# A graph transformer layer and a graph attention layer: three projections by 26 block products instead of three times seven

## The chip, the core and the metric

The kernel runs on one core of a Trainium2 chip. The core has five engines that each work through their own queue of instructions in order and signal each other by semaphores: TensorE (PE, matmuls from SBUF into PSUM; the profile shows its weight loads apart as PEld), VectorE (DVE), ScalarE (ACT), GpSimd (POOL) and SyncE (SP, which here issues nearly all DMAs). The time is device microseconds of one execution, the median of several runs.

## What is computed

128 graphs of 128 nodes with 512 features, all in fp32. Layer 0 normalises, projects to query, key and value, attends over 8 heads with scores that are multiplied by the adjacency matrix, and projects back. Layer 1 is a graph attention layer over the same adjacency. Cut to what matters:

```python
# layer 0
h = jnp.maximum(_layernorm(x), 0.0)
q, k, v = (proj(Wq, bq), proj(Wk, bk), proj(Wv, bv))   # h @ W.T + b, 8 heads of 64
scores = jnp.einsum('bhqd,bhkd->bhqk', q, k) * SCALE
scores = scores * (adj + adj)[:, None, :, :]
ctx = jnp.einsum('bhqk,bhkd->bhqd', softmax(scores), v)
x = x + ctx @ Wo.T + bo
# layer 1
h = jnp.maximum(_layernorm(x), 0.0)
Wh = h @ W
e = leaky_relu(Wh @ a[:512] + (Wh @ a[512:]).T, 0.2)
attention = softmax(where(adj > 0.5, e, -9e15), axis=1)
x = x + elu(attention @ Wh)
```

## The kernel before

Batches (graphs) go in pairs, `p` from 0 to 63, and for the projections in groups `g` of two pairs, four batches. `hA` holds the group's normalised, rectified inputs with features on the partitions, in four blocks: two halves of the tokens (one pair each) by two halves of the features. Each of the products q, k and v is a 2x2 by 2x2 block product by Winograd's scheme: 7 products instead of 8 (`PRODUCTS`, L130), each of 4 matmuls of 256 columns (L258). VectorE forms the sums of weight blocks once (`weight_sum`, L137) and the sums of token blocks for each group (`hidden_sum`, L226, through `token_sum`, L148). The results gather in PSUM banks a, b and c; ScalarE copies a first part out, with the bias for q and k (`firsts`, L281), and VectorE adds the others (`adds`, L285, at L279). The two output projections use the same scheme by rows (`product_rows`, L291).

Around the products, per batch: scores (L320, on half the rows of the TensorE array at a time), weighting by adjacency (L327), maxima, exponentials and shares on VectorE and ScalarE, a blockwise transpose (L355) that goes through DRAM and back (L359, L365), and the context (L388, on half the columns of the array). Per pair: output projection, addition to x (L402), statistics (L165), layer 1 with its two dot products per batch (L425), gathering (L481), projection, elu and store (L511, L515, L521). `hidden` (L217) subtracts the mean and multiplies by the inverse deviation, both read as rows that were sent through DRAM. `shift` (L231) adds a constant row to x.

All work is recorded in an order that is written out by hand: `HEAD`, then `ORDER` once per pair, then `TAIL` are lists of step names with a pair or a lag (L564 to L650), and `steps` (L680) gives each name its function. No scheduler moves anything: each engine runs its instructions in the order in which the steps stand. Step names that matter below: `U`, `F`, `A` the 21 products and their firsts and adds; `hs` the token sums; `hd0`, `hd1` the two halves of `hidden`; `sh` the shift; `cs`, `gs` the token sums of the context `cxT` and of the gathered `gT`; `sca`, `scb` the scores of a pair's two batches and `pca`, `pcb` their contexts. All PSUM tiles come from one pool of 8 banks, taken in turn (L57).

Of the kernel before, what the change touches and what calls it, by code (L numbers as in the profile page):

```python
# [24 lines left out]
def kernel(  # L25
# [6 lines left out]
    wqT: bass.AP,  # L32
    bq: bass.AP,
    wkT: bass.AP,
    bk: bass.AP,
    wvT: bass.AP,
# [23 lines left out]
    xs, x0s, adjs, adjTs, hAs, hSs = {}, {}, {}, {}, {}, {}  # L60
# [18 lines left out]
    def half_of_hidden(p):  # L79

        g, i = divmod(p, 2)
        if g not in hAs:
            hAs[g] = grp.tile([P, 4, 2, 2 * S], F32, name="hA")
        return hAs[g][:, 2 * i : 2 * i + 2].rearrange("p q c k -> p (q c) k")
# [19 lines left out]
    def column(src, name):  # L104
# [10 lines left out]
    wv_sb, wq_sb, wk_sb, wo_sb, w1_sb = (  # L115
        const.tile([P, 7, 2, E // 2], F32, name=name) for name in ("wv", "wq", "wk", "wo", "w1")
    )
# [16 lines left out]
    FIRSTS = {0: (0, 0), 2: (1, 0), 4: (1, 1), 5: (0, 1)}  # L134
    ADDS = {1: (0, 0, "b"), 4: (1, 1, "c"), 6: (1, 0, "c")}
# [12 lines left out]
    def token_sum(h, s, k):  # L148

        if k == 0:  # L150
            nc.vector.tensor_tensor(s[:, 0], h[:, 2], h[:, 3], OP.add)
        elif k == 1:
            nc.vector.tensor_tensor(s[:, 1], s[:, 0], h[:, 0], OP.subtract)  # L153
        elif k == 2:
            nc.vector.tensor_tensor(s[:, 2], h[:, 0], h[:, 2], OP.subtract)
        else:
            nc.vector.tensor_tensor(h[:, 2], h[:, 1], s[:, 1], OP.subtract)
# [59 lines left out]
    def hidden(p, k):  # L217

        h = hAs[p // 2][:, 2 * (p % 2) : 2 * (p % 2) + 2].rearrange("p q c k -> p (q c) k")
        row = rows0[p][:, None, :, k].to_broadcast([P, 2 * 2, 2 * S])  # L220
        if k == 0:
            nc.vector.tensor_tensor(h, h, row, OP.subtract)
        else:
            nc.vector.scalar_tensor_tensor(h, h, 0.0, row, op0=OP.max, op1=OP.mult)

    def hidden_sum(g, k):  # L226
        if g not in hSs:
            hSs[g] = grp.tile([P, 3, 2, 2 * S], F32, name="hS")
        token_sum(hAs[g], hSs[g], k)

    def shift(p):  # L231


        nc.vector.tensor_tensor(xs[p], xs[p], c_sb[:, None, :].to_broadcast([P, 2, E]), OP.add)

    accs = {}

    def product(g, which, n):

        if n == 0:  # L240
            if which == "v":
                vs[g] = grp.tile([P, G, E], F32, name="v")
            else:
                qks[g, which] = {}
        if which != "v" and n in (0, 2):
            qks[g, which][n // 2] = grp.tile([P, C, 2 * S], F32, name=which + "T", bufs=3 if which == "q" else 2)
        w = {"q": wq_sb, "k": wk_sb, "v": wv_sb}[which]
        ha, wb, bank = PRODUCTS[n]
        fresh = (g, which, bank) not in accs
        if fresh:  # L250
            accs[g, which, bank] = ps1.tile([P, 2, 2 * S], F32, name="acc_" + bank, tag="ps1")
        acc = accs[g, which, bank]
        h = hAs[g][:, ha] if ha < 4 else hSs[g][:, ha - 4]
        for m in range(2):
            ms = slice(m * P, (m + 1) * P)
            for c in range(2):
                lhsT, rhs = (h[:, c, ms], w[:, wb, c, :]) if which == "v" else (w[:, wb, c, ms], h[:, c, :])
                nc.tensor.matmul(  # L258
                    acc[:, m, :], lhsT, rhs, start=fresh and m == 0 and c == 0, stop=c == 1, skip_group_check=True
                )  # L260

        def dst(t, f):
            if which == "v":
                return vs[g][:, 2 * t : 2 * t + 2, f * 2 * P : (f + 1) * 2 * P]
            return qks[g, which][t][:, 2 * f : 2 * f + 2, :]

        def first(t, f):
            a = accs[g, which, "a"]
            if which == "v":
                nc.scalar.copy(dst(t, f), a)  # L270
            else:
                bias = bk_sb if which == "k" else bq_sb
                for m in range(2):
                    j = 2 * f + m
                    nc.scalar.activation(dst(t, f)[:, m, :], a[:, m, :], AF.Identity, bias=bias[:, j : j + 1])  # L275

        def add(t, f, bank):
            d = dst(t, f)
            nc.vector.tensor_tensor(d, accs[g, which, bank], d, OP.add)  # L279

        def firsts():  # L281
            if n in FIRSTS:
                first(*FIRSTS[n])

        def adds():  # L285
            if n in ADDS:
                add(*ADDS[n])

        return firsts, adds
# [20 lines left out]
    def scores(b):  # L310
        p, i = divmod(b, 2)
        g, h = divmod(p, 2)
        qT, kT = qks[g, "q"][h], qks[g, "k"][h]
# [80 lines left out]
    def keep_context(b):  # L394
        nc.scalar.copy(rows_of(cxT, b % 2), pcs.pop(b))
# [88 lines left out]
    def keep_gathered(p, i):  # L484
        if p not in gTs:
            gTs[p] = work.tile([P, 7, 2, S], F32, name="gT")
        nc.scalar.copy(rows_of(gTs[p], i), pgs.pop((p, i)))  # L487
# [77 lines left out]
    SEQ = "v0 v1 v2 v3 v4 q0 v5 q1 v6 q2 q3 q4 k0 q5 k1 q6 k2 k3 k4 k5 k6".split()  # L565
# [6 lines left out]
    EARLY, LATE = 3, 4  # L572

    def listed(text, mark):
# [3 lines left out]
        lx@0 lx@1 Lq1@0 Lq0@0 lx@2 Lk0@0 Lk1@0 Lv0@0 t1@-5 Lo0@0 t0@-5 pp@0 hn0@0 hn1@0 tp0@0 t0@-4 tp1@0 ev0@0 ev1@0  # L578
        t1@-4 U6@-2 Wq0@0 pp@1 Wq1@0 t1@-3 U8@-2 hn0@1 l0@-2 Wq2@0 Lv1@0 hn1@1 tp0@1 Lo1@0 U3@-1 Lw1@0 t0@-3 ev0@1 Lu@0
        Wq3@0 pp@2 tp1@1 hn1@2 U5@-1 ev1@1 hn0@2 F6@-2 Wk0@0 hs0@-3 F3@-1 U1@-2 Wk1@0 hs1@-3 hs2@-3 U10@-2 tp0@2 F10@-2  # L580
        U7@-1 t1@-2 t0@-2 U2@-1 Wv0@0 F7@-1 pp@3 Wk3@0 F1@-2 A8@-2 ev0@2 U9@-1 hn0@3 Wv1@0 hn1@3 hs3@-3 tp0@3 l0@-1
        tp1@2 Wv2@0 la@-1 U3@-2 ev1@2 Lw0@0 ev0@3 lt@0 F9@-1 tp1@3 F2@-1 ccp@0 F3@-2 ev1@3 U1@0 ccd@0 t0@-1 t1@-1 U4@-2
        Wo0@0 l0@0 s0@-1 cu10@0 U5@-2 Wv3@0 A5@-1 U4@-1 hs0@-1 U10@-1 U1@-1 F10@-1 F4@-1 ccs@0 A2@-1 cch@0 sca@0 Wk2@0
        scb@0 ata0@0 ata1@0 U6@-1 mxa@0 hs1@-1 exa2@0 U3@1 t1@0 F5@-2 exa3@0 A6@-1 U6@0 A5@-2 F1@0 Wo1@0 rca1@0 t0@0
        U9@-2 F6@0 l0@1 s0@0 exa1@0 f0@0 exa0@0 U3@0 A9@-2 nma3@0 Wo2@0 nma2@0 rca0@0 cu01@0 U10@0 nma1@0 nma0@0 hs2@-1
        F3@1 U8@0 fla@0 Ww0@0 bla@0 U8@-1 atb0@0 la@0 atb1@0 mxb@0 U5@1 A8@0 exb2@0 A9@-1 pla@0 U2@-2 exb0@0 A5@1 exb1@0
        sh@0 F10@0 U11@-1 exb3@0 rcb1@0 U7@-2 nmb3@0 A11@-1 rcb0@0 t0@1 t1@1 U2@1 F7@-2 nmb1@0 cu11@0 l0@2 s0@1 nmb2@0
        f0@1 U7@1 F3@0 lT@0 cu00@0 nmb0@0 lT@1 sca@1 A2@-2 flb@0 scb@1 pca@0 F7@1 ata0@1 blb@0 ata1@1 F2@1 U5@0 mxa@1
        hs3@-1 exa0@1 U9@1 t1@2 exa1@1 Ww2@0 plb@0 exa3@1 t0@2 U1@1 exa2@1 hd0@0 s0@2 F9@1 la@1 U4@1 l0@3 pea@0 rca0@1
        sh@1 hd0@1 U8@1 F4@1 rca1@1 nma1@1 nma0@1 U10@1 A9@1 nma3@1 nma2@1 F5@0 fla@1 o0@0 F10@1 o1@0 atb0@1 bla@1 U4@0  # L590
        atb1@1 mxb@1 pcb@0 od0@0 exb3@1 A5@0 exb0@1 hd1@0 sca@2 pla@1 exb2@1 U9@0 A2@1 exb1@1 Wo3@0 peb@0 rcb0@1 od1@0
        nmb0@1 cs0@0 U11@1 cs1@0 nmb1@1 rcb1@1 cs2@0 nmb2@1 Ww1@0 nmb3@1 cs3@0 o2@0 U2@0 od2@0 flb@1 U6@1 ata0@2 blb@1
        ata1@2 mxa@2 o4@0 o3@0 exa1@2 od4@0 A2@0 exa3@2 U6@2 A6@1 plb@1 exa2@2 od4c@0 hd1@1 o6@0 F6@2 f0@2 hs0@1 o5@0
        exa0@2 A9@0 sup0@0 A11@1 U1@2 rca0@2 od6@0 nma1@2 od5@0 hs2@1 sup1@0 rca1@2 st0@0 nma3@2 U8@2 nma2@2 hs1@1
        nma0@2 st1@0 pca@1 sua0@0 pw@0 pcb@1 pea@1 fla@2 sua1@0 scb@2 peb@1 bla@2 nm@0 F1@2 o0@1 h20@0 atb0@2 atb1@2
        h21@0 U3@2 mxb@2 cs0@1 U7@0 exb3@2 d10@0 exb1@2 d00@0 exb0@2 px@0 U4@2 pd@0 F3@2 la@2 rcb0@2 d01@0 exb2@2 lT@2
        o1@1 rcb1@2 d11@0 nmb2@2 U2@2 od0@1 nmb3@2 cs1@1 nmb1@2 cs2@1 pv@0 cs3@1 nmb0@2 od1@1 U5@2 flb@2 hs3@1 o2@1
        blb@2 F5@2 la@3 o3@1 od2@1 f0@3 A5@2 o4@1 U10@2 od4@1 od4c@1 hd0@2 plb@2 o5@1 wm@0 o6@1 pr@0 F7@0 pla@2 U9@2
        od6@1 od5@1 m1@0 e1@0 U7@2 A9@2 sw@0 st1@1 g0@0 F7@2 st0@1 F10@2 Ww3@0 A2@2 hd1@2
    """  # L600
    ORDER = """
        U1:0 fa:4 ge0:3 pw:2 hs1:1 fb:4 g1:3 nm:2 lT:0 so:4 sca:0 ge1:3 h20:2 scb:0 h21:2 ata0:0 ata1:0 pca:1 mxa:0
# [77 lines left out]
    def steps(p):  # L680
# [21 lines left out]
        for k in range(4):  # L702
            table[f"cs{k}"] = lambda k=k: token_sum(cxT, cxT[:, 4:7], k)
            table[f"gs{k}"] = lambda k=k: token_sum(gTs[p], gTs[p][:, 4:7], k)
# [51 lines left out]
        if odd and (g + 2) * 2 < N:  # L756
            for k in range(4):
                table[f"hs{k}"] = lambda k=k: hidden_sum(g + 2, k)
# [70 lines left out]
```

## Time and profile before

| | |
|---|---|
| median of 3 runs | 2351.22 us (2350.63 to 2351.47) |
| span of the profiled execution, first to last instruction | 2346.1 us |
| matmul records of 256 columns, projections q, k, v | 5376 (2688 matmuls, two records each) |
| matmul records of 256 columns, both output projections | 3584 |
| q, k, v additions on VectorE (L279) | 288, some 680 ns each |
| token sums of hidden on VectorE (L151 to L157, hS) | 128, some 685 ns each |
| mean granted TensorE clock | 0.998 of full speed |

For the profiled execution the page gives only its span; the time of an execution as the runs measure it is 5.1 us longer in the median. The page has one line for busy time, one row of tenths for each engine over 40 slices, the chain of work that ended last (at each step what released it), and groups of equal instructions. An fp32 matmul is two records, each with a weight load. A record's own duration (379 ns for 256 columns) overlaps the next one, so prices are better taken from distances between starts.

### The profile page before, as it was taken

To read this page: it belongs to the slowest core of one execution; us is meant where nothing else is said; L and a number is where in the kernel's file an instruction comes from. 1 tells how busy PE (TensorE), PEld (TensorE's weight loads), DVE (VectorE), ACT (ScalarE), POOL (GpSimd) and SP (SyncE) were. 2 spreads that over 40 slices of the span, in tenths; PEclk is the share of its full clock that TensorE was granted. 3 is DMA by queue.
4 is the path that set the end of the run, shared out by engine and by line. 5 is a ranking of instruction groups with operands and counts; after the bars stand their busy time and mean duration, and the time that the engine had idled before them with its cause. 6 is when DMAs were issued, how large, how long until landed. Compare 5 with 4: busy or idle time off the path is not lost.

```text
span 2346.1 us, 41028 instructions
## 1 busy us (share of the span) xinstructions
PE 2332.0 (99%) x14184; PEld 2061.2 (88%) x14184; DVE 2000.4 (85%) x4113; ACT 1467.2 (63%) x4815; POOL 257.0 (11%) x320
## 2 busy tenths in 40 slices
PE   9999999999999999999999999999999999999998
PEld 8888888888888888888888888888888888888886
DVE  6888888888888888888888888888888888888888
ACT  3656666666566665666666666656666566666774
POOL 1101101111101011011110111110101101110000
PEclk9999999999999999999999999999999999999999
DMA  5445454454444554544535445444454453453332
GB/s 171 131 113 157 121 147 120 124 164 125 143 131 119 148 139 130 143 114 142 155 122 149 120 123 165 124 144 131 120 148 137 131 145 108 146 153 116 118 120 95
DMA packets 267351, 314.06 MB, mean 134 GB/s; under 512 B 24200, under 2 KB 192136, under 8 KB 267144
## 3 DMA queue, kind: packets, MB, share of 16 engines
q1 hardware_dynamic: 263112, 311.31, 45.0%
q8 instruction: 112, 1.84, 0.3%
q0 software_dynamic: 1920, 0.13, 0.2%
q14 instruction: 95, 0.78, 0.1%
q10 hardware_dynamic: 2112, 0.01, 0.1%
HBM read 210.51 MB, written 100.85 MB: 133 GB/s over the span
## 4 chain that ended last, share of the span: by engine, by line
PE 99%; DVE 0%; ACT 0%; DMA 0%; issue 0%; POOL 0%; SPq 0%; ACTq 0%; DVEq 0%; POOLq 0%
PE acc_a L258 29%; PE row_a L299 24%; PE acc_c L258 14%; PE row_c L299 9%; PE acc_b L258 7%; PE sc L320 5%; PE pc L388 5%; PE pg L481 5%; PE pt L197 0%; DMA x<-in_x 0%; PE pm L531 0%; DVE st L165 0%; ACT z L495 0%; PE pu L553 0%; DVE z L499 0%
## 5 line engine op out<-in xcount | busy, mean ns | idle before, releaser
L339 ACT ACTIVATE at<-at,nmx 128x128 f32<-128x128 f32 x1024 | 396.3, 390 | 19.8 <-DVE nmx L334 17.9
L348 ACT ACTIVATE at<-at,rs 128x128 f32<-128x128 f32 x1024 | 325.0, 391 | 12.8 <-DVE rs L343 12.1
L299 PE MATMUL row_a<-wo,cxT 128*128 128x256 f32 x1280 | 328.5, 379 | 0.3 <-DVE cxT L153 0.3
L299 PE MATMUL row_a<-w,gT 128*128 128x256 f32 x1280 | 319.4, 380 | 2.9 <-DVE z L499 1.7
L172 POOL TENSOR_SCALAR mv<-mv 128x2 f32<-128x2 f32 x124 | 79.2, 639 | 2016.8 <-DVE mv L166 1994.6
L299 PEld LDWEIGHTS row_a<-w,gT 128*128 128x128 f32 x1280 | 242.3, 190 | 37.9 <-DVE z L499 2.6
L299 PEld LDWEIGHTS row_a<-wo,cxT 128*128 128x128 f32 x1280 | 242.6, 190 | 34.3 <-DVE cxT L153 0.6
L402 DVE TENSOR_TENSOR x<-row_a,x 128x256 f32<-128x256 f32 x320 | 135.3, 423 | 133.1 <-PE row_a L299 129.8
L495 ACT COPY z<-row_a 128x256 f32<-128x256 f32 x256 | 94.3, 368 | 203.7 <-PE row_a L299 203.6
L275 ACT ACTIVATE kT<-acc_a,bk 128x256 f32<-128x256 f32 x256 | 106.5, 466 | 168.2 <-PE acc_a L258 165.0
L327 DVE SCALAR_TENSOR_TENSOR at<-sc,adj 128x512 f32<-128x512 f32 x256 | 165.1, 686 | 42.2 <-PE sc L320 39.8
L339 ACT ACTIVATION_READ_ACCUMULATOR at<-at,nmx 128x1 f32 x1024 | 193.3, 189 | 0.0
L275 ACT ACTIVATE qT<-acc_a,bq 128x256 f32<-128x256 f32 x256 | 106.1, 466 | 123.0 <-PE acc_a L258 123.0
L165 DVE BATCH_NORM_STATS2 st<-x 128x6 f32<-128x512 f32 x256 | 176.1, 688 | 7.4 <-DMA x<-in_x 5.1
L425 DVE SCALAR_TENSOR_TENSOR junk<-h,u 128x512 f32<-128x512 f32 x256 | 173.3, 677 | 0.6
L355 DVE STREAM_TRANSPOSE tr<-at 128x1024 f32<-128x1024 f32 x128 | 158.8, 1240 | 9.2 <-PE pc L388 2.7
L334 DVE TENSOR_REDUCE nmx<-at 128x8 f32<-128x1024 f32 x128 | 156.2, 1220 | 4.3
L487 ACT COPY gT<-pg 128x512 f32<-128x512 f32 x128 | 74.6, 584 | 123.8 <-PE pg L481 117.4
L481 PEld LDWEIGHTS pg<-w,h 128*128 128x128 f32 x1024 | 133.3, 192 | 6.6 <-ACT z L495 0.2
L173 POOL TENSOR_TENSOR mv<-mv,mhalf 128x2 f32<-128x2 f32 x128 | 131.1, 1024 | 30.7 <-DVE mv L168 20.3
L481 PE MATMUL pg<-w,h 128*128 128x128 f32 x1024 | 134.1, 275 | 0.0
L299 PE MATMUL row_c<-w,gT 128*128 128x256 f32 x512 | 133.0, 382 | 0.6 <-DVE z L499 0.5
(130 smaller groups left out, 4876.4 us busy)
## 6 DMA issues: line engine op xcount, KB each, us to landing
blocks<-tr SPq DMA_DIRECT2D x128, 512.0 KB, 6.8
aT<-blocks SPq DMA_DIRECT2D x512, 128.0 KB, 2.9
x<-in_x SPq DMA_DIRECT2D x123, 512.0 KB, 5.0
out<-x SPq DMA_DIRECT2D x63, 512.0 KB, 4.1
hA<-in_xT SPq DMA_DIRECT2D x120, 256.0 KB, 3.7
mr<-rows SPq DMA_DIRECT2D x60, 256.0 KB, 4.4
adj<-in_adj SPq DMA_DIRECT2D x64, 128.0 KB, 4.3
adjT<-in_adjT SPq DMA_DIRECT2D x64, 128.0 KB, 4.2
```

What stands on the lines that cost most here:

```text
L165: nc.vector.bn_stats(st, src[:, i, :])
L258: nc.tensor.matmul(acc[:, m, :], lhsT, rhs, start=fresh and m == 0 and c == 0, stop=c == 1, skip_group_check=True)
L275: nc.scalar.activation(dst(t, f)[:, m, :], a[:, m, :], AF.Identity, bias=bias[:, j : j + 1])
L299: nc.tensor.matmul(acc, left[:, la, c, :], w[:, wb, c, :], start=n in (0, 3) and c == 0, stop=c == 1, skip_group_check=True)
L327: nc.vector.scalar_tensor_tensor(ats[b][0][:, k * C : (k + 1) * C, :], scs[b][k], QSCALE, adjs[p][:, i : i + 1, :].to_broadcast([P, C, S]) ...
L334: nc.vector.tensor_reduce(nmx, at, AX.X, OP.max, negate=True)
L339: nc.scalar.activation(at[:, j, :], at[:, j, :], AF.Exp, bias=nmx[:, j : j + 1], accum_out=sums[:, j : j + 1])
L348: nc.scalar.activation(at[:, j, :], at[:, j, :], AF.Copy, scale=rs[:, j : j + 1])
L355: nc.vector.transpose(trs[b], at.rearrange("p h (j k) -> p j h k", k=Q))
L402: nc.vector.tensor_tensor(d, row_acc(p, "o", bank), d, OP.add)
L425: nc.vector.scalar_tensor_tensor(junk, h2[:, i, :], 1.0, u_sb[:, k, :], op0=OP.mult, op1=OP.mult, accum_out=ws[:, i, 1:2] if k else src_sb ...
L481: nc.tensor.matmul(pg[:, c, :], h1s[p][0][:, i, c * P : (c + 1) * P], wts[p][:, i, :], start=True, stop=True)
```

## The change

The three projections become one bilinear scheme for a 2x4 by 4x4 block product with 26 products. The weights of q, k and v lie side by side (`w_sb`, 28 slots of 3 x 128 columns); 35 sums over them (`WSUMS`) are made once, at the start, on VectorE. For each group 17 sums of token blocks (`FORMS`, 128x256) are made on GpSimd and are shared by q, k and v. A product (`TERMS`: chain, form, weight slot, where its result goes) is two matmuls of 256 columns for query and key (`product_qk`) and two of 128 for value (`product_v`). Products of one chain add up in one PSUM bank, and the bank is read between them: 24 of 26 products are followed by a take, which is a copy by ScalarE for the first of each of 8 output blocks and an addition or subtraction by VectorE for the other 16, apart for query with key and for value.

Also: `hidden`'s subtraction and `shift` go from VectorE to GpSimd, in halves; the token sums of context and gathered read two of their blocks from PSUM; `ORDER` is now run once per group instead of once per pair; and all three lists are new. The output projections, the attention and layer 1 are otherwise as before.

```diff
-    FIRSTS = {0: (0, 0), 2: (1, 0), 4: (1, 1), 5: (0, 1)}
-    ADDS = {1: (0, 0, "b"), 4: (1, 1, "c"), 6: (1, 0, "c")}
+    TERMS = list(terms("""
+        1,8,7,13- 0,10,18,10- 1,9,19,03- 0,11,0,00- 1,1,20,01+ 0,2,16,. 1,13,5,11+ 0,0,21,03- 1,12,6,12- 0,0,1,02-
...
+    FORMS = list(sums("""
+        4+5 1-8 2+9 0+9 5+7 12-1 3-13 1+2 6+12 16-15 17-3 0-18 16+19 6+19 4-19 7-17 5-1
+    """))
...
+    def load_blocks(n):
+        nc.sync.dma_start(w_sb[:, n : C * C : C], wT[:, n : C * C : C])
+    def block_sum(k):
+        d, a, op, b = WSUMS[k]
...
-            nc.vector.tensor_tensor(s[:, 1], s[:, 0], h[:, 0], OP.subtract)
+            nc.vector.tensor_tensor(s[:, 1], s[:, 0], block(0), OP.subtract)
...
         if k == 0:
-            nc.vector.tensor_tensor(h, h, row, OP.subtract)
+            for c in range(0, C, 2):
+                nc.gpsimd.tensor_tensor(h[:, c : c + 2], h[:, c : c + 2], row[:, c : c + 2], OP.subtract)
...
-        nc.vector.tensor_tensor(xs[p], xs[p], c_sb[:, None, :].to_broadcast([P, 2, E]), OP.add)
+        for i in range(2):
+            nc.gpsimd.tensor_tensor(xs[p][:, i, :], xs[p][:, i, :], c_sb, OP.add)
...
+    def make_form(g, k):
+        a, op, b = FORMS[k]
+        forms[g, 2 * C + k] = grp.tile([P, 2 * S], F32, name="tf", bufs=8)
+        eng = nc.gpsimd
+        eng.tensor_tensor(forms[g, 2 * C + k], form(g, a), form(g, b), OP.add if op == "+" else OP.subtract)
...
+    def product_qk(g, n):
+        _, f, slot, _ = TERMS[n]
+        acc, fresh = fresh_acc(g, n, "q", [P, 2, 2 * S])
+        for i in range(2):
+            nc.tensor.matmul(
+                acc[:, i, :], w_sb[:, slot, i, :], form(g, f), start=fresh and i == 0, stop=True, skip_group_check=True
+            )
+    def product_v(g, n):
+        _, f, slot, _ = TERMS[n]
+        acc, fresh = fresh_acc(g, n, "v", [P, 2, P])
+        for i in range(2):
+            nc.tensor.matmul(
+                acc[:, i, :], form(g, f)[:, i * P : (i + 1) * P], w_sb[:, slot, 2, :],
+                start=fresh and i == 0, stop=True, skip_group_check=True,
+            )
+    def take_qk(g, n):
+        chain, _, _, (t, j, sign) = TERMS[n]
+        acc = accs[g, chain, "q"]
...
+        if (g, t, j) not in begun:
+            begun.add((g, t, j))
+            for i, bias in enumerate((bq_sb, bk_sb)):
+                nc.scalar.activation(d[:, i, :], acc[:, i, :], AF.Identity, bias=bias[:, j : j + 1], scale=float(sign))
+        else:
+            nc.vector.tensor_tensor(d, d, acc, OP.add if sign > 0 else OP.subtract)
+    def take_v(g, n):
...
+            nc.scalar.activation(d, acc, AF.Copy, scale=float(sign))
+        else:
+            nc.vector.tensor_tensor(d, d, acc, OP.add if sign > 0 else OP.subtract)
...
-        for p in range(EARLY, N - LATE):
+        for g in range(EARLY, N // 2 - LATE):
             for step, lag in ORDER:
-                if p >= lag:
-                    do(step, p - lag)
+                do(step, 2 * g - lag)
```

In the lists, `L` and `W` are now the loads and sums of weight blocks, `T` the forms, `Q` and `V` the products, `A` and `B` their takes.

## The prediction

> **What bounds the kernel now.** I read the page first: busy shares, the slices, then the chain that ended last.
>
> ```profile
> PE 2332.0 (99%) x14184; PEld 2061.2 (88%) x14184; DVE 2000.4 (85%) x4113; ACT 1467.2 (63%) x4815; POOL 257.0 (11%) x320
> ...
> PE   9999999999999999999999999999999999999998
> ...
> PE 99%; DVE 0%; ACT 0%; DMA 0%; issue 0%; POOL 0%; SPq 0%; ACTq 0%; DVEq 0%; POOLq 0%
> PE acc_a L258 29%; PE row_a L299 24%; PE acc_c L258 14%; PE row_c L299 9%; PE acc_b L258 7%; PE sc L320 5%; PE pc L388 5%; PE pg L481 5%; PE pt L197 0%; DMA x<-in_x 0%; PE pm L531 0%; DVE st L165 0%; ACT z L495 0%; PE pu L553 0%; DVE z L499 0%
> ```
>
> TensorE is the bound in every slice, and half of the chain (29+14+7%) is the query, key and value products of line 258, which the change replaces. VectorE, at 85%, is next. Second, the stretches view (us, then busy us per engine):
>
> ```profile
> 0.00:20.00 20.00, 14.82 (x69) 12.92 (x70) 11.85 (x30) 3.80 (x6) 3.66 (x11) 0.83 0.93 309
> 1000.00:1073.00 73.00, 73.00 (x450) 64.81 (x449) 62.80 (x130) 46.35 (x152) 8.36 (x11) 1.00 0.46 137
> ```
>
> In the steady state TensorE never stops; 5.2 us of its 14 us of idling are in the first 20. Third, the chain in order of time gives prices that don't depend on overlapping records:
>
> ```profile
> 1036.21 1.73 PE acc_a L258 x8
> 1037.93 0.89 PE pg L481 x8
> 1038.83 1.99 PE sc L320 x32
> 1040.81 1.90 PE pc L388 x32
> 1042.71 1.92 PE acc_c L258 x8
> 1044.63 1.73 PE acc_b L258 x8
> ```
>
> Each matmul is two records. Eight records of 256 columns take 1.73, so one such matmul 0.4325; eight of 128 columns (pg) take 0.89, so 0.2225 each. The block after pc takes 1.92 instead of 1.73: going from the split array (sc uses 64 rows, pc 64 columns) back to the whole costs 0.19. The pieces elsewhere agree: 16 sc records 1.09 and 32 of them 1.99, so 0.90 per 16 and 0.19 for entering; pc 1.02 and 1.90 likewise. The same chain shows one block recurring at 441.21 and 513.42: the period of one group of four batches is 72.21.
>
> Fourth, what VectorE waits for in 1000 to 1073, and one place of the GpSimd and VectorE timelines:
>
> ```profile
> DVE x L402 <- PE row_a L299: 4.7, 5, 2.0
> DVE x L234 <- DMA x<-in_x: 1.6, 1, 1.6
> DVE at L327 <- PE sc L320: 1.3, 2, 0.9
> DVE nmr L412 <- POOL mv L173: 0.6, 1, 0.6
> DVE z L499 <- ACT z L495: 0.5, 1, 0.5
> DVE rs L343 <- ACT at L339: 0.2, 1, 0.2
> ```
>
> The six sum to 8.9, so VectorE is taken for 64.1 of 73, or 63.4 of the 72.21.
>
> ```profile
> 1000.50 1.19 DVE L511 SCALAR_TENSOR_TENSOR x<-z,x 128x1024 f32<-128x1024 f32 x1
> 1001.80 1.23 DVE L515 SCALAR_TENSOR_TENSOR x<-ez,x 128x1024 f32<-128x1024 f32 x1
> ...
> 1000.76 1.02 POOL L172 TENSOR_SCALAR mv<-mv 128x2 f32<-128x2 f32 x1 [22.97 <-DVE mv L166]
> 1001.86 1.75 POOL L173 TENSOR_TENSOR mv<-mv,mhalf 128x2 f32<-128x2 f32 x1
> ...
> 1011.88 0.30 POOL L172 TENSOR_SCALAR mv<-mv 128x2 f32<-128x2 f32 x1 [8.27 <-DVE mv L166]
> 1012.26 0.70 POOL L173 TENSOR_TENSOR mv<-mv,mhalf 128x2 f32<-128x2 f32 x1
> ```
>
> GpSimd's two small steps take 0.30 and 0.70 when alone, but 1.02 and 1.75 when VectorE is in an instruction with two SBUF inputs: both end only after VectorE does.
>
> [...] VectorE's 512-element rows (683 ns) recur every 0.60.
>
> **The change part by part**, per group of four batches, of which there are 32.
>
> *TensorE, products.* Removed: 3 x 7 products x 4 matmuls of 256 columns = 84 x 0.4325 = 36.3. Added: 26 products, each 2 matmuls of 256 columns (query, key) and 2 of 128 (value): 52 x 0.4325 + 52 x 0.2225 = 22.5 + 11.6 = 34.1. Gain 2.27, x 32 = 72.6. The value price is that of pg, same shape; the bounds are half of a 256-column matmul (0.216: 11 us better in all) [...]. I take 0.2225, because pg runs eight in a row with a load for each at that price.
>
> *TensorE, splits.* In the built order of instructions the array changes between whole, row-split and column-split 205 times before and 328 times after: a pair of batches went sc, pc, whole (3 changes), and now goes pc, sc, whole, sc, whole (5). 123 x 0.19 = 23.4 lost. Net on TensorE: 72.6 - 23.4 = 49 gained; the period goes to 72.21 - 2.27 + 4 x 0.19 = 70.7.
>
> *VectorE.* Prices are distances between starts: 1.14 for 1024 elements, 0.60 for 512, 0.34 for 256. Removed: two shifts and two subtractions of the mean (4 x 1.14), four token sums (4 x 0.60), nine additions to q, k and v (9 x 0.60): 12.4. Added: of 24 takes 8 are firsts on ScalarE, so 16 x 0.60 + 16 x 0.34 = 15.0. Taken: 63.4 + 2.7 = 66.1 of 70.7, or 94%. It still fits, with 4.6 to spare instead of 8.8. The token sums of cxT and gT now read one input from PSUM at the same size: nothing to gain or lose beyond 0.03 each.
>
> *ScalarE.* Query and key stay 16 pieces; value goes from 4 x 0.58 to 8 x 0.37: +0.6, in 25 us of slack. Nothing.
>
> *GpSimd.* Added: 17 forms of 256 elements, 4 + 4 halves of 512: [...] What queues behind a form there are the other forms, mv (L173) and its DMA, all ordered well ahead.
>
> [...] In a group VectorE has 20 instructions with two SBUF inputs left (8 dots, 2 hidden, 4 of fa/fb, 6 small). [...] I charge 0.2 per period for late additions that TensorE then meets: 6 in all, bounds 0 and 30.
>
> *The start.* Weight sums for q, k and v: 12 x 0.60 = 7.2 before; now 35 of 384 elements, about 0.47 each (between 0.34 and 0.60): 16.5. Counting both engines' work by these prices along the emitted order: at the 175th matmul TensorE has 42 us of work, VectorE 50 (before: 48 and 36). VectorE starts at 5.1, when x lands, so TensorE can't be there before 55, minus the few us that an addition may lag: it idles about 13 instead of 5. Cost +8, bounds +2 and +16. DMA carries as much as before (3.1 MB of weights), the first block row before the rest; SP's queue has 820 rows for 822.
>
> *The end.* The same last rows, elu and stores; 0, bounds -2 and +5.
>
> Sum against the span: 2346.1 - 49 + 8 + 6 = 2311. The median of the runs, 2351.2, lies 5.1 above the span: 2316.
>
> **The rivals.**
>
> *A, forecast (0.52).* As above; by the bounds of the value price, start and small stalls 2296 to 2336.
>
> *B, waits inside the chains take the gain (0.17).* A bank is now read while its chain goes on: some 20 times per group and for both kinds the next matmul of a chain waits until the addition before it has read the bank, and that addition stands in VectorE's queue, now 94% full. If one wait in ten is late by 0.35, it is 4 x 0.35 = 1.4 per group, 42 in all: 2316 - 6 + 30 to 42 = 2340 to 2352. For it: VectorE's small spare. Against: before, nine additions of this kind cost TensorE nothing, and takes and next terms stand some steps apart.
>
> *C, [...] (0.20), slower.* Place: the 20 two-input instructions. Each us of blocking above 4.6 per group lengthens the period by one. After the start's 8, the gain is used up at a period of 72.1, so at 6 us of blocking, 0.24 for each of the 25 GpSimd instructions. At 7.5 the period is 73.6 and the time 2316 - 6 + 30 x 2.9 = 2397. For it: the 1.02 and 1.75 rows, which show the block is whole. Against: 24 two-input instructions of VectorE per group are gone (8) or now read PSUM (16 token sums).
>
> *D, better (0.06).* Value at 0.216, the start hidden: below 2296.
>
> *E, another order cost (0.05),* a late x or aT in SP's queue: 2345 to 2365. That the change leaves TensorE's work alone can be excluded: the built program has 3456 matmuls of 256 columns for 4480, and 2264 of 128 for 600.
>
> **How the numbers follow.** 0.2% (4.7 us) is about what a measurement can tell from no change. Faster: A 0.52, D 0.06, and most of B, 0.13: 0.71. Same: 0.04 of B, 0.02 of E: 0.06. Slower: C 0.20, E 0.03: 0.23. The predicted time is A's. The range from 2294 to 2362 takes in A, B, most of E and the light end of C, and leaves out D's better half and C's heavy part.
>
> **What would show it.** Right: a period of 70.7 to 71; eight 128-column value records near 0.89; some 328 pieces with 0.19; VectorE busy 93 to 97%; TensorE idling near 13 us at the start. Wrong: VectorE's two-input rows (dots 677 ns, fa/fb 1.2 us) longer on average, TensorE waiting for v or qk additions in the steady state, a period over 72.

## The result, and the profile after

The median of 7 runs is 2342.42 us (2340.49 to 2347.51), against 2351.22 us for 7 runs of the kernel before on the same chip: a ratio of 0.9967, 95% interval 0.9956 to 0.9977. The change makes the kernel 0.33% faster: 8 to 9 us, where the forecast was 35. The profiled execution has a span of 2338.7 us, where the forecast's sum was 2311. So about 27 us of the expected gain are not there, and the rest of this text looks for them.

The page of the kernel after, busy shares first, then the slices of TensorE and the chain that ended last by engine:

```profile
PE 2311.8 (99%) x15464; PEld 2048.8 (88%) x15464; DVE 2106.2 (90%) x4620; ACT 1470.5 (63%) x4943; POOL 963.5 (41%) x1112
...
PE   8999999999999999999999999999999999999998
...
PE 95%; DVE 2%; DMA 1%; POOL 1%; ACT 1%; issue 1%; SPq 0%; POOLq 0%; DVEq 0%; ACTq 0%
```

TensorE is still the bound, but 5% of the chain now lies on other engines, where it was about 1%. The view by stretches (us, then busy us and records of PE, PEld, DVE, ACT and POOL, granted clock, DMA share, GB/s) of the two stretches that the prediction showed:

```profile
0.00:20.00 20.00, 10.99 (x46) 9.43 (x47) 12.58 (x34) 3.67 (x5) 7.77 (x18) 0.80 0.89 295
1000.00:1073.00 73.00, 72.98 (x495) 65.12 (x494) 66.38 (x147) 46.43 (x157) 31.04 (x37) 1.00 0.46 141
```

In the steady state TensorE is busy in 72.98 of 73 us, and yet the period is 71.31 us (one block of products recurs at 288.16, 359.46 and 430.77 in the chain of waits) and not the 70.7 that was worked out. A busy share can't show why: a record that starts a fraction of a microsecond late still counts as busy, because the record before it is drawn out or overlaps it (one of 256 columns is shown with 0.38 us, and the next starts after 0.216). So I took from the trace, for every TensorE record, the distance to the start of the next one less the price of its shape (0.216 us for 256 columns; 0.112 for 128, or for two records on a split array) and less the cost of a change between the whole and a split array (0.197 us by the same distances). What is left, where it is more than 0.01 us, I add up and call stalls:

| stalls of TensorE, us | 0 to 217 us | 217 to 2200 | 2200 to the end | sum |
|---|---|---|---|---|
| before | 8.1 | 1.4 | 6.9 | 16.4 |
| after | 27.5 | 16.0 | 11.9 | 55.4 |
| more | 19.4 | 14.6 | 5.0 | 39.0 |
| charged in the prediction | 8 | 6 | 0 | 14 |

39.0 us of new stalls against a charge of 14: that is 25 of the missing 27 us. What remains after the stalls, TensorE's work proper, fell from 2329.7 to 2283.3 us, so by 46.4; 49 were forecast. The work was read rightly, the stalls were not. In every kernel below the same subtraction gives 2283 to 2284 us of work (e3_warm apart, with 38 more transposes), so the stalls alone tell the kernels apart.

### The profile page after: what moved, and what is told of

The parts are those of the page before. It is cut to its first block, busy times and chain, and to the rows that moved or that the text cites. A ratio compares the mean times of both kernels' runs of the same rounds, so it can differ in the third digit from the quotient of the medians.

```text
span 2338.7 us, 45871 instructions
## 1 busy us (share of the span) xinstructions
PE 2311.8 (99%) x15464; PEld 2048.8 (88%) x15464; DVE 2106.2 (90%) x4620; ACT 1470.5 (63%) x4943; POOL 963.5 (41%) x1112
## 4 chain that ended last, share of the span: by engine, by line
PE 95%; DVE 2%; DMA 1%; POOL 1%; ACT 1%; issue 1%; SPq 0%; POOLq 0%; DVEq 0%; ACTq 0%
PE acc_q L297 31%; PE row_a L346 23%; PE acc_v L306 16%; PE row_c L346 9%; PE sc L367 6%; PE pc L435 5%; PE pg L528 5%; DMA x<-in_x 0%; DMA mr<-rows 0%; DVE st L205 0%; DVE x L449 0%; DVE junk L472 0%; POOL hA L263 0%; PE pm L578 0%; POOL mv L213 0%
## 5 line engine op out<-in xcount | busy, mean ns | idle before, releaser
L297 PE MATMUL acc_q<-tf,w 128*128 128x256 f32 x2176 | 554.3, 384 | 3.6 <-DVE w L170 2.7
L282 POOL TENSOR_TENSOR tf<-hA,tf 128x256 f32<-128x256 f32 x288 | 254.7, 889 | 645.6 <-PE acc_v L306 616.5
L297 PEld LDWEIGHTS acc_q<-tf,w 128*128 128x128 f32 x2176 | 392.0, 191 | 59.4 <-issue 5.3
L323 DVE TENSOR_TENSOR qk<-qk,acc_q 128x512 f32<-128x512 f32 x512 | 341.4, 677 | 69.4 <-PE acc_q L297 69.0
L306 PEld LDWEIGHTS acc_v<-w,tf 128*128 128x128 f32 x2176 | 318.9, 191 | 27.0 <-PE row_a L346 0.9
L306 PE MATMUL acc_v<-w,tf 128*128 128x128 f32 x2176 | 325.8, 275 | 0.7 <-DVE at L374 0.6
L297 PE MATMUL acc_q<-hA,w 128*128 128x256 f32 x1152 | 298.4, 382 | 0.9 <-ACT qk L321 0.9
L297 PEld LDWEIGHTS acc_q<-hA,w 128*128 128x128 f32 x1152 | 211.0, 190 | 35.6 <-DVE qk L323 8.9
L336 DVE TENSOR_TENSOR v<-v,acc_v 128x256 f32<-128x256 f32 x512 | 205.8, 407 | 27.6 <-PE acc_v L306 27.3
L263 POOL TENSOR_TENSOR hA<-hA,mr 128x512 f32<-128x512 f32 x120 | 164.6, 1392 | 134.7 <-DMA mr<-rows 130.2
L270 POOL TENSOR_TENSOR x<-x,c 128x512 f32<-128x512 f32 x128 | 160.9, 1277 | 139.7 <-ACT qk L321 65.9
```

The costliest lines, as they stand in the source:

```text
L263: nc.gpsimd.tensor_tensor(h[:, c : c + 2], h[:, c : c + 2], row[:, c : c + 2], OP.subtract)
L270: nc.gpsimd.tensor_tensor(xs[p][:, i, :], xs[p][:, i, :], c_sb, OP.add)
L282: eng.tensor_tensor(forms[g, 2 * C + k], form(g, a), form(g, b), OP.add if op == "+" else OP.subtract)
L297: nc.tensor.matmul(acc[:, i, :], w_sb[:, slot, i, :], form(g, f), start=fresh and i == 0, stop=True, skip_group_check=True)
L306: nc.tensor.matmul(acc[:, i, :], form(g, f)[:, i * P : (i + 1) * P], w_sb[:, slot, 2, :], start=fresh and i == 0, stop=True, skip_group_ch ...
L323: nc.vector.tensor_tensor(d, d, acc, OP.add if sign > 0 else OP.subtract)
```

## Where the steady state loses half a microsecond per period

In each period the same few places carry the stalls. This is one of them in the chain of waits of the kernel after, in order of time (start, us, what), and ScalarE's timeline at the same moment:

```profile
1053.12 1.73 PE row_a L346 x8
1054.85 0.44 PE acc_v L306 x4
1055.29 0.02 issue
1055.31 1.13 PE row_a L346 x4
```

```profile
1054.89 0.37 ACT L542 COPY z<-row_a 128x256 f32<-128x256 f32 x1 [2.85 <-PE row_a L346]
```

The second row_a piece (step `w5`) writes the bank that the first one (`w4`) filled, and in between ScalarE must copy it to z. That takes from 1054.89 to 1055.26, and the only piece between, a value product, lasts 0.44 us. ScalarE stood idle and waiting for 2.85 us before it: no queue is late. The view shows the wait as 0.02 us, because a record's own duration reaches over its gap, but it costs 0.28: the next record starts 0.18 late behind acc_v, and the first record of row_a takes 0.10 longer. (The chain shows 1.13 for that piece where 0.86 is the price: 0.10 is this, and the rest is that the view draws its last record to its own end, which overlaps the next piece.) A second place, at 1008.3, costs 0.18. TensorE's and VectorE's timelines there:

```profile
1007.64 1.03 PE L346 MATMUL row_a<-w,gT 128*128 128x256 f32 x4
1008.58 0.48 PE L297 MATMUL acc_q<-hA,w 128*128 128x256 f32 x1
```

```profile
1007.84 0.69 DVE L323 TENSOR_TENSOR qk<-qk,acc_q 128x512 f32<-128x512 f32 x1 [0.57 <-PE acc_q L297]
```

`Q12` (1008.58) follows `Q11` in its chain with one piece of 0.86 us (`w0`, from 1007.64) between. The addition of `A11` on VectorE starts 0.20 after `w0` does, which is when the records of `Q11` are through, and takes 0.69; `Q12` starts 0.05 after its end. Together that is 0.94, so 0.08 more than the piece between, and `Q12`'s first record takes 0.10 longer. VectorE too had been waiting before, for 0.57 us. Small ones at 1012.2 and 1017.5 bring the sum to 0.56 us per period, 0.51 more than in the kernel before.

The theory for the experiments: it is the order of steps. Pieces are short now, above all the value products with half the columns, and one of them, 0.44 us long, no longer covers the read of a bank between two products of a chain. The rival: GpSimd's work makes VectorE late in general, and the stalls only show it.

## Experiments

All are edits of the kernel after, timed beside the kernel before. As a landmark inside the executions I use the start of the 17th of VectorE's 128 blockwise transposes (L402): 338.9 us after, read from VectorE's timeline. One execution of each kernel was traced, and how far two differ by chance can be seen where the orders are the same. e8_tail has the order of the kernel after up to TAIL, and e9_tail2 that of e6_order; yet their landmarks come 2.6 and 2.4 us later, and their steady states have 2.9 and 4.1 us more of stalls. So a difference of this size between two traces shows nothing. The diffs show parts of the lines of the lists.

**e1_gap.** Two moves of steps.

```diff
-        w0:2 exa3:-1 B8:0 Q12:0 A12:0 V10:0 zc0:2
+        w0:2 exa3:-1 B8:0 V10:0 Q12:0 A12:0 zc0:2
...
-        cs2:1 Q3:0 o1:1 zc2:3 w4:3 fla:0 zc4:3 lT:-1 V1:0 bla:0 w5:3
+        cs2:1 o1:1 zc2:3 V1:0 w4:3 fla:0 zc4:3 lT:-1 Q3:0 bla:0 w5:3
```

> Two moves of steps in ORDER, so that between two products of one chain a longer piece stands while the bank is read. Theory (short pieces between chained products): of the 0.51 us that TensorE loses per period, 0.47 goes; period 71.31 to 70.85, over some 27 periods 12 to 13 us, so about 2330 (ratio to the kernel before 0.991). Rival (VectorE is late [...]): the waits turn up at the next place; period stays at 71.2 or more, gain under 3 us.

Measured: 2338.61 us (2334.79 to 2340.18), ratio 0.9942 (0.9929 to 0.9956). The period is 71.05, and stalls between 217 and 2200 us fell from 16.0 to 9.9. Both repaired places are gone, but a new one of the same kind came up: `w4` waits 0.2 us for `zc2`, which stands on ScalarE behind exponentials and a 512-element activation. By the stalls that is half of the expected gain, by the medians a third (3.8 us), and a hint of how thin the margins are: what was gained at one place makes the next one late.

**e6_order.** The same two moves, and two more, which take up what e1_gap left.

```diff
-        w2:2 nma0:-1 h20:1 d00:1 exa2:-1 nma1:-1 w3:2 rca1:-1 B10:0 V15:0 zc2:2 h21:1
+        w2:2 nma0:-1 h20:1 d00:1 zc2:2 exa2:-1 nma1:-1 w3:2 rca1:-1 B10:0 V15:0 h21:1
...
-        Q17:0 exb0:-1 Q14:0 A14:0 px:1 wd4c:2 V17:0 o0:0 w1:2
+        Q17:0 w1:2 exb0:-1 Q14:0 A14:0 px:1 wd4c:2 V17:0 o0:0
```

> The two moves of the run before, and two more in ORDER: zc2 ahead of exa2 on ScalarE, w1 between Q17 and Q14. Theory (each stall is a piece that is too short for the read of a bank, and repairs expose the next one): period 71.05 to 70.75, time 2330 to 2333. Rival (VectorE or ScalarE is simply late on average, repairs only move the stall): period stays at 71.0 or more, 2337 to 2340.

Measured: 2329.26 us (2325.72 to 2331.59), ratio 0.9906 (0.9893 to 0.9920). The period is 70.75 in most of the run, with single ones of up to 72.0, and stalls between 217 and 2200 us are 4.0. The chain of waits at the place shown above, in e6_order:

```profile
1044.51 2.79 PE row_a L346 x12
1047.30 0.44 PE acc_v L306 x4
1047.74 0.87 PE row_a L346 x4
1048.61 0.86 PE acc_q L297 x4
```

Each piece has the price of its shape (2.79 is 12 x 0.216 and the change from the split array). After `w4` (1047.74) comes `Q3`, 0.86 us long, and there is no wait line any more. Four moves of steps, with every instruction of the change kept, return 13 us, 12 of them in the stalls of the steady state; the interval doesn't touch that of the kernel after. The rival's prediction for this run (71.0 or more) is refuted. This is the fastest version that leaves nothing out: 0.9% faster than the kernel before.

**e2_pool.** Nearly all of GpSimd's work left out, and with it the sums of token blocks.

```diff
-        return hAs[g][:, k] if k < 2 * C else forms[g, k]
+        return hAs[g][:, k] if k < 2 * C else form(g, FORMS[k - 2 * C][0])
...
-                nc.gpsimd.tensor_tensor(h[:, c : c + 2], h[:, c : c + 2], row[:, c : c + 2], OP.subtract)
+                nc.gpsimd.tensor_tensor(h[:, c, 0:2], h[:, c, 0:2], row[:, c, 0:2], OP.subtract)
...
-            nc.gpsimd.tensor_tensor(xs[p][:, i, :], xs[p][:, i, :], c_sb, OP.add)
+            nc.gpsimd.tensor_tensor(xs[p][:, i, 0:2], xs[p][:, i, 0:2], c_sb[:, 0:2], OP.add)
```

> Left out: the sums of token blocks (products read the first block of each sum instead), and hidden's subtraction and shift work on 2 columns only. GpSimd has next to nothing to do, and no product waits for a form. Theory: VectorE's two-input rows go back (dots 764 to some 680 ns), but the period keeps its 0.5 us of stalls (71.2 or more); only the start and the last rows gain, up to 8 us: 2334 to 2342. Rival ([...]): period 70.8 or less and 2315 to 2322.

Measured: 2382.2 us (2378.97 to 2386.3), ratio 1.0131 (1.0117 to 1.0145), slower than both. Neither theory had that. The chain of waits of one period shows what the edit did besides:

```profile
1069.39 6.42 DMA mr<-rows
1075.81 0.42 DVE x L446
1076.22 0.61 DVE at L371
1076.83 0.14 issue
1076.97 0.68 PE acc_v L303 x4
```

The chain names the load of mr, but the queues show another one. SyncE's issues of loads, and then GpSimd's `shift` (L270) and `hidden` (L263), at the same place:

```profile
1066.94 1.69 SPq L115 DMA_DIRECT2D hA<-in_xT  x2
1068.74 0.55 SPq L98 DMA_DIRECT2D x<-in_x  x1
1069.39 0.41 SPq L253 DMA_DIRECT2D mr<-rows  x1
```

```profile
1075.58 0.34 POOL L270 TENSOR_TENSOR x<-x,c 128x2 f32<-128x2 f32 x2 [8.60 <-ACT qk L318]
1076.34 0.35 POOL L263 TENSOR_TENSOR hA<-hA,mr 128x2 f32<-128x2 f32 x2 [0.42 <-DMA mr<-rows]
```

With the products reading hA themselves, its buffer comes free only at a group's last product. The load of the next xT waits for that at the head of SyncE's queue, and the load of x, queued behind it, is late: its last part lands at 1075.45. `shift` on GpSimd waits for x, and VectorE's addition to x (1075.81) for `shift`. The load of mr can't be what it waited for: it ends at 1076.18, and `hidden`, which reads it, stands behind `shift`. So the run doesn't tell the theories apart. It shows something else: the sums of blocks are also copies that free hA early.

**e7_port.** The same question without that side effect: one sum is made and all products that want a sum read that one; `hidden` and `shift` as in e2_pool.

```diff
-        forms[g, 2 * C + k] = grp.tile([P, 2 * S], F32, name="tf", bufs=8)
-        eng = nc.gpsimd
-        eng.tensor_tensor(forms[g, 2 * C + k], form(g, a), form(g, b), OP.add if op == "+" else OP.subtract)
+        if not forms:
+            one = const.tile([P, 2 * S], F32, name="tf")
+            nc.gpsimd.tensor_tensor(one, form(g, a), form(g, b), OP.add if op == "+" else OP.subtract)
+            forms["one"] = one
+        forms[g, 2 * C + k] = forms["one"]
```

> Left out: all sums of token blocks but the very first (products read that one block of real data in their place), and hidden's subtraction and shift work on 2 columns only. Unlike the run before, hA is not held longer, so no load gets late. Theory: VectorE's dots go from 764 back to some 685 ns, but the period keeps its stalls, 71.2 or more; the start gains some 4 us: 2336 to 2340. Rival ([...]): period 70.8 or less, 2322 to 2328.

Measured: 2333.59 us (2332.49 to 2337.7), ratio 0.9929 (0.9916 to 0.9941). Groups of instructions by line and shape (busy us, mean ns of one, idle before it), in the kernel after and then in e7_port, the dot products and the weight sums:

```profile
L472 DVE SCALAR_TENSOR_TENSOR junk<-h,u 128x512 f32<-128x512 f32 x256 | 195.7, 764 | 7.2 <-ACT h L465 1.6
L170 DVE TENSOR_TENSOR w<-w 128x384 f32<-128x384 f32 x26 | 16.1, 641 | 0.2
```

```profile
L474 DVE SCALAR_TENSOR_TENSOR junk<-h,u 128x512 f32<-128x512 f32 x256 | 176.1, 688 | 7.3 <-ACT h L467 1.7
L170 DVE TENSOR_TENSOR w<-w 128x384 f32<-128x384 f32 x26 | 13.8, 552 | 1.7 <-DMA w<-in_wT 1.6
```

GpSimd's work does cost VectorE time: 764 against 688 ns for a dot product, 641 against 552 for a weight sum. With `fa` and `fb` (1296 and 1304 against 1215 and 1217) and the scaling of w (490 against 425), each times its count, that is some 34 us in all beside the weight sums, 1.1 per group. The additions that read PSUM take as long in both kernels, 677 ns for query and key and 407 for value. But the period only goes from 71.31 to 71.24, and the stalls of the two places shown above are still there with 0.28 and 0.18. The first of them in the chain of waits of e7_port:

```profile
1048.95 0.44 PE acc_v L308 x4
1049.39 0.02 issue
1049.41 1.13 PE row_a L348 x4
```

Most of what is gained lies at the start: the landmark comes at 333.7 instead of 338.9, 5.2 us. Some 3 us lie in the steady state, where stalls go from 16.0 to 13.0: besides the 0.07 per period, no single period is late any more (the longest is 71.30; in the kernel after one is 72.27).

**e5_nowsum.** The weight sums left out.

```diff
     def block_sum(k):
+        return
...
-                acc[:, i, :], w_sb[:, slot, i, :], form(g, f), start=fresh and i == 0, stop=True, skip_group_check=True
+                acc[:, i, :], w_sb[:, loaded(slot), i, :], form(g, f), start=fresh and i == 0, stop=True, skip_group_check=True
```

> Left out: the 35 sums of weight blocks (a product reads the first loaded block that its slot was to be summed from). Theory (VectorE's queue sets the start): 35 x some 0.47 = 16.5 us of VectorE's work goes from the first 150 us; TensorE's stalls before 217 us, 19.4 more than in the kernel before, fall by 8 to 12, and the time to 2330 to 2334. Rival (loads of x and weights, GpSimd's forms [...] set the start): gain under 3 us, 2339 or more.

Measured: 2338.18 us (2335.84 to 2341.34), ratio 0.9946 (0.9932 to 0.9959). The stretch from 20 to 60 us, in the kernel after and then in e5_nowsum, columns as above:

```profile
20.00:60.00 40.00, 38.46 (x230) 32.97 (x229) 37.93 (x75) 13.92 (x40) 19.31 (x25) 0.97 0.32 96
```

```profile
20.00:60.00 40.00, 38.94 (x253) 33.91 (x252) 25.40 (x55) 15.75 (x51) 18.89 (x27) 1.00 0.34 98
```

VectorE, 95% busy in the kernel after, has 12.5 us less to do, and TensorE gets through 253 records instead of 230. The landmark comes 6.4 us earlier, and stalls before 217 us are 20.9 instead of 27.5. That is under the 8 to 12 expected, and only 4.2 us are left at the end: the steady state and the end have 1.5 and 2.1 us more of stalls than the kernel after. That is no more than two traces of one order differ by.

**e3_warm and e4_pm: the clock.** In the kernel after, TensorE's clock is granted at half in parts of the first 23 us (8.7 to 15.5 and 19.0 to 22.4) and again around 91 to 97 us. The first begins in an idle time of 4.5 us after the warm-up transposes, the last comes in the run of 16 matmuls with one column each (pm, L578). This stretch, columns as above, has a clock of 0.66:

```profile
90.00:100.00 10.00, 10.00 (x57) 9.09 (x58) 6.58 (x15) 4.15 (x18) 1.74 (x2) 0.66 0.50 144
```

The edits: `range(62)` for `range(24)` in `warm_up`, and `product_c` in four parts, behind the products `Q12`, `Q17`, `V12` and `V17` in HEAD.

> 62 warm-up transposes instead of 24, so that TensorE has work until about 10 us. Theory: the granted clock stays at 1.0 from 10 to 24 us, where it was 0.5 at times; TensorE's half-speed records cost 4.5 us there, but weight sums stand close behind, so 1 to 3 us of gain: 2339 to 2341. Rival (VectorE alone sets the start): clock up, gain under 1 us.

> The 16 matmuls of one column (pm, product_c) go in four parts between products instead of in one run of 3.5 us. Theory: the clock no longer halves at 90 to 97 us; pc there takes 1.02 instead of 1.90, pu 0.44 instead of 0.91, and 2 to 3.6 us are gained: 2339 to 2340. Rival (the waits for VectorE at 127 and 132 us stand fixed): TensorE waits there longer instead, gain under 1 us.

Measured: e3_warm 2344.5 us (2342.93 to 2346.63), ratio 0.9972 (0.9962 to 0.9983); e4_pm 2342.08 us (2340.94 to 2345.86), ratio 0.9962 (0.9949 to 0.9974). Neither can be told from the kernel after. Nor did e3_warm do what it was made for. Two stretches of it:

```profile
10.00:20.00 10.00, 4.88 (x30) 3.77 (x29) 7.79 (x22) 2.17 (x4) 5.52 (x8) 0.84 1.01 358
20.00:25.00 5.00, 3.95 (x12) 2.78 (x12) 5.00 (x10) 2.79 (x7) 3.83 (x4) 0.65 0.01 4
```

The first idle time is filled, and stalls in the first 20 us fell from 12.8 to 8.8 us. But TensorE then waits 3.9 us for a weight sum at 15.0, and the half clock comes at 16.7 to 23.5 instead; the landmark moved by 1.2 only. In e4_pm the pieces of pm ran at full clock (1.00 from 85 to 94 us), then the context piece waited 1.5 us, and the half clock came behind that instead, from 95.7 to 99.1; the landmark is 1.8 us later. Both differences are within what two traces of one order differ by. In both runs the half clock came later and for 3.4 us less, but it did not go, so what it costs isn't shown.

**e8_tail and e9_tail2: the end.** The largest stall there, 2.2 us at 2276.5, in the chain of waits of the kernel after:

```profile
2274.00 1.11 POOL mv L212
2275.11 0.07 issue
2275.18 1.68 POOL mv L213
...
2278.60 0.27 ACT z L542
2278.86 0.04 issue
2278.91 1.13 PE row_a L346 x4
```

GpSimd's two small steps take 1.11 and 1.68 us here, where they take 0.22 and 0.72 in the median of this kernel. VectorE is in `fa` and `fb` meanwhile (from 2273.83 and 2275.06, 1.19 and 1.22 us long), and both steps end only after those. The copy z stands behind the two steps `h2` on ScalarE, which wait for the small steps. e8_tail moves `fa`, `fb` and `so` behind `nm`:

```diff
-        pw@-3 fa@-5 exa0@-1 exa1@-1 rca0@-1 g0@-4 ge0@-4 pca@-2 pea@-2 exa2@-1 fb@-5 so@-5 nm@-3
+        pw@-3 exa0@-1 exa1@-1 rca0@-1 g0@-4 ge0@-4 pca@-2 pea@-2 exa2@-1 nm@-3 fa@-5 fb@-5 so@-5
```

> In TAIL fa and fb of one pair, two VectorE instructions with two SBUF inputs, stand behind nm instead of between the statistics and nm. Theory ([...] GpSimd's two small steps, 1.11 and 1.68 us there): these take some 0.3 and 0.7, TensorE's wait of 2.2 us at 2276.5 falls to under 0.6, time 2340 to 2341. Rival (another chain ends right behind): wait still over 1.5, no gain.

Measured: 2342.94 us (2342.35 to 2346.44), ratio 0.9968 (0.9955 to 0.9980). The same two lines of the chain in e8_tail:

```profile
2279.43 0.23 POOL mv L212
2279.66 0.07 issue
2279.73 0.72 POOL mv L213
```

The small steps take 0.23 and 0.72, as expected, but TensorE's stall is still 2.1 us: `fa` and `fb` now stand ahead of the sums of gT on VectorE, and `w2` waits for these. In e9_tail2, on top of e6_order, five copies `zc0` go ahead of the `h2` steps:

```diff
-        w0@-4 V24@-4 w1@-4 h21@-3 gs1@-4 d10@-3 h20@-3 d00@-3 zc0@-4 w2@-4
+        w0@-4 V24@-4 w1@-4 zc0@-4 h21@-3 gs1@-4 d10@-3 h20@-3 d00@-3 w2@-4
```

> The order of e6_order, and in TAIL the copy zc0 of five pairs stands ahead of the h2 steps on ScalarE, which wait for the statistics by way of GpSimd. Theory (in the last rows w2 waits only because zc0 is queued behind h2): TensorE's 2.0 us wait for z goes, and 1.5 to 3 us of e6_order's 2329.3: 2326 to 2328. Rival (VectorE is the bound of the last 60 us, 93% busy there): the wait turns up at the next product, gain under 0.7 us.

Measured: 2333.83 us (2328.3 to 2336.09), ratio 0.9921 (0.9908 to 0.9933): no gain over e6_order, if anything a loss, and the intervals overlap. The waits of TensorE from 2245 us on, in e9_tail2 (who waited for whom: sum, times, longest):

```profile
PE row_a L346 <- ACT z L542: 1.4, 3, 0.5
PE row_a L346 <- DVE gT L193: 1.3, 1, 1.3
```

The wait for z fell from 3.4 (e6_order) to 1.4, and 1.3 for the sums of gT came in its place. From the 121st transpose to the end both kernels take the same 148.2 us. The traced execution of e9_tail2 is 6.4 us longer than that of e6_order, but all of it lies ahead of the end: 4.1 us of stalls in the steady state and 2.6 at the start, in steps that the two have in common. Two links of the chain at the end were taken out, and each time another VectorE queue stood behind.

**e11_hn.** On top of e6_order, six of the eight normalisations before the first transposes go to ScalarE, which is little used at the start (3.67 us of the first 20 in the kernel after).

```diff
+            nc.vector.scalar_tensor_tensor(nmr, mv[:, :, 0], -1.0, mv[:, :, 1], op0=OP.mult, op1=OP.mult)
...
+            nc.scalar.activation(hns[p][:, i, :], src[:, i, :], AF.Identity, bias=nmr[:, i : i + 1], scale=mv[:, i, 1:2])
```

> The order of e6_order, and for the pairs 0, 2 and 3 the normalisation before the transposes goes from VectorE (6 x 0.46) to ScalarE, with one small step (3 x 0.1) on VectorE for its bias. Theory (VectorE's queue sets the start): 1 to 2.5 us gained, 2327 to 2328. Rival (ScalarE's longer way, statistics to bias to copy, comes late): no gain or up to 1 us lost.

Measured: 2334.22 us (2329.33 to 2334.98), ratio 0.9922 (0.9909 to 0.9936); the landmark is 0.3 us earlier than in e6_order, the profiled span the same 2327.5. No gain, which speaks against VectorE's sum of work as the only bound of the start; but the 1 to 2.5 us that were expected are no more than two traces differ by.

**e10_all.** The new order, and the weight sums and nearly all of GpSimd's work left out: the edits of e6_order, e5_nowsum and e7_port together.

> The order of e6_order; left out: the 35 weight sums (as in e5_nowsum), and all GpSimd work but the first sum of token blocks and 2 columns of hidden's subtraction and of shift (as in e7_port). Theory (order, weight sums and GpSimd's work are three separate terms, 13.1, 6.4 and 5.2 us by the runs so far): period 70.75, landmark after 17 batches at 325 to 328 us for 338.9, and 2316 to 2319. Rival (they overlap: one takes the place of another): 2323 or more.

Measured: 2313.21 us (2310.89 to 2316.3), ratio 0.9836 (0.9822 to 0.9849). The period is 70.75 over the whole steady state, with 0.1 us of stalls in all between 217 and 2200 us; stalls before 217 us are 13.4, the landmark is at 324.1. The three terms add up: 14.9 us at the landmark, where e6_order, e5_nowsum and e7_port gave 1.7, 6.4 and 5.2, together 13.3. The end keeps its stalls, 12.1 us.

## Why the prediction was right and wrong

The part that failed is the count of TensorE's stalls: 14 us were charged, and 39.0 are there. The saving in TensorE's work, 46.4 us for 49, was right. Term by term:

- *TensorE, products:* right. Four records of 128 columns take 0.44 to 0.45 us, the price that was taken from pg; the bound at half the price of 256 columns, 0.43 for the four, did not come true.
- *TensorE, splits:* right. A change between array modes costs 0.197 us by the trace (0.093 and 0.100 at the way in, 0.097 and 0.104 at the way out of 16 score records, two changes). The pieces of pc, 1.02 and 1.90, give 0.14 and not the 0.19 that was read from them; the distances between starts settle it. With both terms, the period of 70.7 is what e10_all and most of e6_order show.
- *VectorE:* right in kind. It is busy for 66.4 of 73 us, 91%, a little under the 93 to 97 named (these counted from start to start, which before gave 64.1 for 62.8 busy). It isn't the bound in the steady state.
- *ScalarE, "nothing":* right for its load, wrong as a step. With 25 us of slack in a period, its copies still decide two of the stalls (`w5` after `zc4`, 0.28 us, and in e1_gap `w4` after `zc2`, 0.2), because what matters is when the copy can start and what stands ahead of it in order.
- *GpSimd:* it is no bound, busy for 31.0 us in 73. What the added work would take was the author's estimate: the kernel before has no GpSimd addition of this size that could give a price. In the stretch shown above the added work takes 24.9 us (sums of token blocks 14.7, the halves 10.2), and the small steps that were there before, with their DMA, 6.1 where they took 8.4. A 256-element addition takes 0.73 us in the median and 0.72 at the least, or 2.8 to 2.9 ns per element, and up to 1.73.
- *Late additions, 0.2 per period, 6 in all:* the charge was the author's estimate, and it is the step that failed in the steady state. What it was meant for is small: GpSimd's work costs VectorE 1.1 us per group, and the period 0.07. The traces show the delay on both sides: 764 instead of 688 ns for VectorE's dot products, 1.11 and 1.68 us instead of 0.22 and 0.72 for GpSimd's small steps. But the new stalls in the steady state, for which this term stood, are 14.6 us and have another cause: places in ORDER where one short piece separates two products of a chain. e6_order shows it by taking 12 of the 14.6 away with four moves. The rest are single late periods, which e7_port and e10_all, without GpSimd's work, don't have.
- *The start, +8:* the term was too small by 11, the largest miss of all. There are 19.4 us of new stalls, of which weight sums carry 6.6 (27.5 to 20.9) and GpSimd's work 5.5 (27.5 to 22.0), by the experiments; together with the order 14.1. The count of VectorE's load against TensorE's had the weight sums in it, but at 16.5 us; in the trace they keep VectorE busy for 21.0 (16.1 for the 26 shown above, 4.9 for the other nine). GpSimd's work wasn't in the count. What the clock costs, which the prediction didn't have either, isn't shown. The rest, some 5 us, stays open.
- *The end, 0:* wrong by 5, at the edge of its bounds. TensorE meets VectorE's queue (the statistics, the sums of gT, additions to x) more often in the new order of TAIL. e8_tail and e9_tail2 took out two links and gained nothing, e10_all keeps the loss without GpSimd's work. Which order would return it is open.
- *Rivals:* B had the right kind of wait with the wrong reason: not one in ten takes late in VectorE's queue, but a few fixed places, each time, where the engine that reads the bank had been waiting; 0.51 us per period instead of 1.4. That its 2340 to 2352 takes in the measured time is luck: it puts 30 to 42 us into the steady state, where 14.6 are, and the rest came at the start and the end. C, in which GpSimd's work makes VectorE the bound, is refuted by the period of 71.31 and by e7_port. The "against" that was written for B, that takes and next terms stand some steps apart, was never counted in the built order of instructions; at these places it was one step. And the costliest place isn't in the new chains at all, but in the output projection, of which the change altered only the order.

## What to carry to other kernels

When products are split into smaller ones that share a PSUM bank, count for each pair of neighbours in a chain how many microseconds of other work stand between, and compare that with what the read of the bank takes: until the records are through, the read itself, and the start of the next product (here 0.20 + 0.69 + 0.05 us on VectorE, 0.21 + 0.37 + 0.05 on ScalarE). TensorE, 99% busy, still lost 0.7% of its period here in waits of which a view shows one as 0.02 us that cost 0.28: sum the distances between starts against prices, place by place. And after a repair look at the next place before the gain is called small: by the stalls of the steady state the first two moves here gave 6 us, and two more gave 6 again.

## What the runs showed of the hardware that had not been expected

- A TensorE wait that the view shows as 0.02 us (1055.29 in the kernel after) cost 0.28: the record before it is followed 0.18 us late, and the first record after it takes 0.10 longer.
- The clock fell to half in a stretch in which TensorE was never idle, in the run of 16 matmuls with one column each (0.50 between 91 and 97 us). The run lasted some 4.5 us there; in the kernel before it took 3.5 us (32.9 to 36.4), at a clock of 1.00. What makes the difference, no run here shows.
- Two loads issued one behind the other landed late in single periods. In e9_tail2 at 831 us the loads of x and mr took 8.8 and 8.5 us; in the period before 5.1 and 5.8. In the new kernel `shift` waits on GpSimd for x, `hidden` stands behind it, and VectorE waits for both: TensorE then stalls by about 1 us, twice. e7_port and e10_all, with GpSimd's work gone, have no such period. Why the loads are late at times isn't shown.
